# Transformer block with expert routing on one core: new places for the last sequences, a search with both candidates at hand, adds by half

## Chip, cores and metric

The kernel runs on one core of a Trainium2 chip. The metric is the device time of one execution in microseconds; the time before is the median of 3 runs. All 128 partitions are used, all data is float32 unless said otherwise.

## What is computed

```
x: 16 sequences x 256 tokens x 256;   H=16 heads of 64;   E=8 experts, hidden 1024
h     = layernorm(x)*g + b + silu(t) @ W_ada.T + b_ada
q,k,v = h @ Wqkv.T ;  q, k normalised per head
x     = x + softmax(q k' / 8) v @ Wout.T
gate  = softmax(x @ Wgate.T)                   # 4096 tokens x 8 experts
vals, idx = top_k(gate.T, 4096/8)              # every expert takes its 512 best tokens
y     = gelu(layernorm(x[idx]) @ fc1.T + b1) @ fc2.T + b2
out   = x.at[idx].add(y * vals)
```

The choice of the experts needs the gates of all tokens, so it can't begin in full before the last sequence is through the attention.

## The kernel before

**Stages.** The first part works through 16 sequences of 256 tokens (two tiles of 128). For each one `First` normalises and transposes x; `Group` (b, g, t) makes one 512-wide block g of q, k or v for tile t, groups 0 to 3 with square, sum, power (POOL), scaling and transposes, groups 4 and 5 (the values) with a copy alone; `Quad` (b, d) handles four heads in two pairs i of two heads j: scores (TensorE, PE in the profile), maxima (VectorE, DVE), exponentials (ScalarE, ACT), normalising (GpSimd, POOL), transposes, copies and the product with v; `Tail` (b, t) projects, adds x, writes the result to `out` and its normalised form to `xn_dram`, and computes the gates of the tile. In `EARLY` sequences three quarters of the projection are issued ahead of the rest.

**Two routings.** Each expert's 512 tokens are found in two halves of 256. The `first` routing uses the gates of tiles 0 to 29 alone (sequences 0 to 14), so it can run beside the attention of sequence 15; the `second` uses all tiles without those chosen. There are 16 jobs (lines 862 to 985), eight experts for each routing. A job compares places with a row of lane numbers (`onehot`, 30 or 32 tiles), turns that into a list of 256 token numbers with small matmuls (`list_matmul`, `take`), gathers their rows (`gather`, two indirect DMAs issued by POOL), transposes them, runs `up`, `gelu`, `down`, `finish` in two halves i of 128 tokens, and adds each half to `out` (`scatter`, an indirect DMA with addition, issued by POOL).

**The search** (lines 773 to 798) finds for every expert the bits of the value that 256 gates reach, in 30 steps from bit 29 to bit 0. `compare` counts on each partition how many of 256 values reach the candidate, `count` adds up the 16 partitions of an expert with a 128x128 matmul, `drop` turns a count below 255.5 into the bit to take back, and `step` takes it back and sets the next one. All four follow from each other. `masks`, `totals`, `place`, `turn_places` and `split` then give every token its place in the list.

**The order.** Within the first part and up to the first job, the order in which each engine gets its work is written out by hand. Every step has a place, a number; the steps are sorted by it (line 1068) and issued in that order, and each engine takes its own in that order. The numbers give the order alone, they set no times. `STEADY` (line 137) has the places of one sequence, shifted by `PERIOD` for each; `START` and `END` (lines 182 and 252) replace parts of them for the first and last sequences; `GATES`, `TURN`, `SEARCH`, `PLACE`, `LIST`, `UP`, `DOWN` and `SCATTER` (lines 332 to 372) have those of the routing and the first job. The jobs from 1 on run in a loop of 16 slots each (line 1101), with the second routing's steps, the next job's lists and its gather laid into the slots.

**Buffers** are rings: a tile takes the next buffer of its tag and waits until the last readers of it are done. Tags that matter here: `mm` (3 PSUM banks: projections, transposes, counts), `sc` (4: scores and transposed scores), `po` (1), and in SBUF `pr` (6: exponentials), `prT` (5: their transposes), `tok` (2), `xn` (3).

Of the kernel before, what the change touches and what calls it, by code (L numbers as in the profile page):

```python
# [18 lines left out]
P = 128  # L19
# [7 lines left out]
TB = N // P  # L27
# [16 lines left out]
def kernel(  # L44
# [35 lines left out]
    def rsqrt(dst, src):  # L80
# [13 lines left out]
    )  # L94
    below = const.tile([P, P], BF16, name="below")
# [156 lines left out]
    END = {  # L252
        13: dict(
            tail=((785.465, 790.273, 798.692, 815.100, 809.231, 833.838, 858.249, 860.611), (801.111, 811.928, 832.334, 851.976, 852.521, 857.274, 860.648, 863.953)),
        ),
        14: dict(
            quad={
                (0, 0): (778.689, 786.219, 823.152),
                (0, 0, 0): (779.682, 781.429, 786.791, 815.299, 818.486),
                (0, 0, 1): (785.912, 785.925, 792.535, 808.580, 817.952),  # L260
                (0, 1): (780.096, 783.733, 823.483),
                (0, 1, 0): (781.545, 781.892, 784.628, 788.947, 788.970),
                (0, 1, 1): (780.101, 782.800, 786.708, 786.733, 788.171),
                (1, 0): (797.364, 818.438, 836.328),
                (1, 0, 0): (800.501, 805.864, 819.296, 829.860, 830.258),
                (1, 0, 1): (800.411, 814.443, 822.953, 828.276, 828.813),
                (1, 1): (793.490, 829.748, 838.784),
                (1, 1, 0): (796.388, 796.418, 830.890, 834.362, 838.122),
                (1, 1, 1): (808.778, 813.542, 829.820, 831.934, 838.359),
                (2, 0): (820.804, 836.676, 852.048),  # L270
                (2, 0, 0): (828.203, 828.813, 838.415, 843.722, 847.331),
                (2, 0, 1): (827.939, 828.914, 836.722, 843.910, 849.000),
                (2, 1): (836.374, 842.713, 852.072),
                (2, 1, 0): (836.407, 839.805, 842.769, 848.474, 850.007),
                (2, 1, 1): (839.520, 841.416, 848.115, 848.519, 850.465),
                (3, 0): (816.908, 832.905, 857.083),
                (3, 0, 0): (825.275, 825.873, 838.515, 849.510, 853.000),
                (3, 0, 1): (827.433, 827.464, 834.209, 851.571, 852.526),
                (3, 1): (838.557, 848.820, 857.138),
                (3, 1, 0): (842.137, 843.903, 849.558, 853.124, 855.600),  # L280
                (3, 1, 1): (838.661, 846.376, 854.896, 856.165, 856.629),
            },
            out=(833.850, 847.258, 852.123, 857.223),
            tail=((862.946, 865.847, 868.980, 875.067, 865.880, 866.612, 872.508, 873.385), (858.831, 861.745, 877.140, 877.177, 862.888, 865.191, 867.264, 869.065)),
        ),
        15: dict(
            group={
                (0, 0): (783.010, 784.168, 792.362, 806.317, 814.099, 816.308, 819.667, 798.729),
                (0, 1): (830.066, 833.953, 850.378, 857.740, 857.952, 870.574, 874.791, 839.548),
                (1, 0): (879.001, 881.846, 885.813, 890.395, 890.820, 899.277, 903.588, 882.489),  # L290
                (1, 1): (873.858, 878.170, 878.690, 878.937, 883.088, 887.096, 887.770, 879.768),
                (2, 0): (846.402, 853.106, 854.291, 858.091, 859.371, 870.406, 875.263, 852.946),
                (2, 1): (840.588, 856.986, 858.168, 861.123, 862.155, 868.313, 873.733, 844.023),
                (3, 0): (890.733, 891.793, 895.647, 895.684, 895.713, 917.885, 917.990, 894.050),
                (3, 1): (881.675, 882.780, 889.034, 892.080, 894.627, 906.787, 911.766, 884.681),
                (4, 0): (888.740, 890.011),
                (4, 1): (863.214, 868.004),
                (5, 0): (923.865, 925.480),
                (5, 1): (924.711, 926.046),
            },  # L300
            quad={
                (0, 0): (877.464, 881.499, 926.628),
                (0, 0, 0): (879.672, 880.455, 885.321, 920.421, 922.538),
                (0, 0, 1): (879.870, 880.809, 887.655, 912.768, 921.958),
                (0, 1): (877.518, 892.971, 933.343),
                (0, 1, 0): (886.956, 891.463, 894.729, 911.136, 911.826),
                (0, 1, 1): (880.898, 888.187, 894.314, 911.428, 916.354),
                (1, 0): (895.648, 919.627, 937.995),
                (1, 0, 0): (898.733, 909.723, 928.093, 930.689, 932.290),
                (1, 0, 1): (910.215, 915.043, 924.694, 928.544, 932.034),  # L310
                (1, 1): (886.728, 916.952, 939.979),
                (1, 1, 0): (887.974, 905.007, 923.144, 927.338, 929.333),
                (1, 1, 1): (892.287, 897.473, 926.382, 928.417, 929.117),
                (2, 0): (923.105, 929.115, 953.105),
                (2, 0, 0): (923.819, 925.246, 929.628, 941.427, 943.494),
                (2, 0, 1): (926.871, 927.001, 942.982, 945.434, 945.886),
                (2, 1): (921.492, 928.553, 954.846),
                (2, 1, 0): (926.000, 926.034, 939.614, 940.072, 943.252),
                (2, 1, 1): (924.318, 925.786, 942.242, 945.444, 951.283),
                (3, 0): (931.133, 940.346, 955.254),  # L320
                (3, 0, 0): (936.244, 936.261, 940.865, 941.536, 950.189),
                (3, 0, 1): (933.464, 935.504, 943.785, 944.131, 949.789),
                (3, 1): (937.165, 948.250, 957.499),
                (3, 1, 0): (938.436, 940.374, 948.920, 954.409, 955.964),
                (3, 1, 1): (940.955, 942.777, 948.685, 953.607, 955.715),
            },
            out=(934.112, 945.132, 954.889, 957.518),
            tail=((961.580, 961.705, 961.951, 972.971, 962.994, 969.038, 969.773, 970.133), (961.977, 963.425, 970.214, 973.543, 969.153, 973.476, 975.274, 976.692)),
        ),
    }  # L330
    EARLY = {14: (859.048, 858.196,), 15: (957.531, 960.238,)}
    GATES = ((865.946, 872.056, 872.537, 895.813,), (873.513, 875.766, 877.480, 896.008,))
    TURN = (877.896, 880.780,)
    LOAD = (862.948, 961.979)
    SEARCH = (
        (880.819, 881.055, 881.404, 881.710), (882.829, 883.509, 886.236, 886.333),
        (887.758, 887.777, 888.291, 888.656), (888.696, 889.378, 891.481, 891.532),
        (891.823, 892.179, 892.583, 894.026), (895.504, 895.899, 896.433, 897.275),
        (897.999, 902.133, 902.702, 903.674), (910.101, 910.322, 914.650, 914.946),
        (915.318, 915.341, 915.350, 915.983), (916.961, 917.286, 917.306, 918.504),  # L340
        (919.277, 920.204, 920.381, 920.683), (920.702, 920.727, 920.758, 921.907),
        (922.078, 922.144, 922.719, 922.794), (923.075, 923.211, 923.878, 923.905),
        (924.099, 924.525, 925.286, 925.814), (925.990, 926.221, 926.333, 926.641),
        (926.653, 927.067, 927.185, 927.194), (927.246, 928.070, 928.254, 928.471),
        (929.054, 929.057, 929.362, 929.575), (930.411, 931.087, 931.232, 931.596),
        (932.027, 932.536, 932.959, 933.097), (933.383, 933.445, 933.785, 934.727),
        (934.977, 937.418, 937.926, 938.225), (938.272, 939.383, 939.547, 940.683),
        (940.952, 940.980, 941.209, 942.937), (942.957, 942.999, 943.081, 943.091),
        (943.308, 943.939, 944.131, 944.157), (944.158, 944.713, 948.920, 948.933),
        (949.194, 950.535, 950.850, 950.862), (951.462, 952.102, 952.117, 952.284),  # L350
    )
    PLACE = (952.741, 953.958, 955.045, 956.213, 956.540, 970.822,)
    LIST = (
        dict(gives=957.438, onehot=(956.590, 957.558, 956.649, 957.964, 958.690, 958.856,),
             matmul=(957.536, 958.538, 958.607, 958.768, 958.802, 959.218,),
             then=(959.465, 959.489, 962.176, 962.208,)),
        dict(gives=958.877, onehot=(959.876, 961.470, 960.649, 958.698, 962.036, 961.622,),
             matmul=(960.722, 961.809, 961.857, 962.038, 963.442, 963.636,),
             then=(965.066, 965.769, 967.569, 971.532,)),
    )  # L360
    UP = (
# [827 lines left out]
```

## Time and profile before

| | us |
|---|---|
| median of 3 runs | 1214.87 (1214.84 to 1214.93) |
| the profiled execution | 1212.76 |
| its span, first to last instruction | 1210.8 |
| PE busy | 1168.7 (97%) |
| DVE, ACT, POOL busy | 764.4, 618.2, 591.3 |
| first search, first comparison to the masks | 879.68 to 927.14 |
| first `up` matmul of job 0 | 949.43 |

The page divides the span into 40 equal slices of some 30 us. A digit is the busy share of an engine in tenths; `PEclk` is the clock that TensorE was granted. Every row of a timeline has its start in us from the span's start, its length, the engine, the line of the kernel, the operation, and in brackets the idle time ahead of it with what ended that. PEld is the load of a matmul's stationary operand, which may run beside the matmul before.

### The profile page before, as it was taken

The numbers are of one execution on the slowest core, as the hardware profiler recorded it, in microseconds if no ns is written. First come the engines' busy times: TensorE is split into PE (matmuls) and PEld (weight loads), VectorE is DVE, ScalarE is ACT, GpSimd is POOL, SyncE is SP. The second block draws the span as 40 slices with busy tenths as digits, with TensorE's granted clock in tenths as the row PEclk, the third lists the DMA queues.
The fourth block names the chain that finished last, engine by engine and source line by source line (L and its number), as shares of the span: only waits on it lengthen the run. The fifth ranks groups of instructions, "written<-read, shape, count | busy, mean of one in ns | idle before, by whom it ended". The sixth has DMA issues, their size and how long they took to land. (4 is left out here: it accounts for less than half of the span.)

```text
span 1210.8 us, 19463 instructions
## 1 busy us (share of the span) xinstructions
PE 1168.7 (97%) x6784; PEld 813.0 (67%) x6784; DVE 764.4 (63%) x2244; ACT 618.2 (51%) x1701; POOL 591.3 (49%) x818
## 2 busy tenths in 40 slices
PE   6999999999999999999999999999987989999996
PEld 3556666667575666666666657567744778888885
DVE  7656665757665656666575666565578557875541
ACT  2665565555555555556555555556564233333331
POOL 4654555545455555555554545555574233333332
PEclk9999999999999999999999999999989899999999
DMA  5000000000000000000000000000200356666661
GB/s 184 1 1 5 22 6 23 9 18 14 14 14 14 27 1 27 6 22 6 22 10 18 14 14 14 14 19 14 97 0 2 114 178 182 179 182 181 183 184 25
DMA packets 46738, 62.40 MB, mean 52 GB/s; under 512 B 3888, under 2 KB 39984, under 8 KB 46640
## 3 DMA queue, kind: packets, MB, share of 16 engines
q1 hardware_dynamic: 39808, 52.70, 12.8%
q0 software_dynamic: 6144, 8.39, 3.8%
q8 instruction: 54, 0.88, 0.3%
q14 instruction: 44, 0.36, 0.1%
q10 hardware_dynamic: 688, 0.06, 0.0%
HBM read 48.56 MB, written 12.58 MB: 50 GB/s over the span
## 5 line engine op out<-in xcount | busy, mean ns | idle before, releaser
L608 POOL TENSOR_SCALAR pr<-pr,sums 128x256 f32<-128x256 f32 x512 | 238.7, 484 | 277.1 <-DVE sums L604 258.7
L506 PE MATMUL pm<-wq,hT 128*128 128x512 f32 x768 | 355.0, 601 | 5.2 <-DMA wq<-in_wqkvT 3.1
L597 ACT ACTIVATE pr<-sc,nmax 128x256 f32<-128x256 f32 x512 | 236.4, 476 | 162.8 <-DVE nmax L588 148.3
L82 POOL TENSOR_TENSOR ss<-ss,neghalf 128x8 f32<-128x8 f32 x128 | 210.4, 1648 | 96.0 <-DVE ss L527 93.2
L506 PEld LDWEIGHTS pm<-wq,hT 128*128 128x128 f32 x768 | 137.5, 191 | 147.7 <-issue 137.5
L588 DVE TENSOR_REDUCE nmax<-sc 128x2 f32<-128x512 f32 x256 | 164.6, 682 | 45.6 <-PE sc L581 45.5
L523 DVE TENSOR_REDUCE ss<-sq 128x8 f32<-128x512 f32 x128 | 87.4, 683 | 106.0 <-ACT sq L519 105.9
L617 PEld LDWEIGHTS pp<-ident,pr 128*128 128x128 f32 x1024 | 118.3, 143 | 34.9 <-issue 19.6
L617 PE MATMUL pp<-ident,pr 128*128 128x128 f32 x1024 | 137.6, 274 | 3.3 <-ACT pr L597 2.5
L635 PE MATMUL po<-prT,v 128*64 128x256 f32 x1024 | 137.6, 391 | 0.7 <-ACT oT L645 0.7
L581 PE MATMUL sc<-kT,qT 64*128 64x256 f32 x1024 | 131.2, 394 | 0.0
L519 ACT ACTIVATE sq<-pm 128x512 f32<-128x512 f32 x128 | 77.1, 602 | 90.5 <-PE pm L506 89.3
L659 PE MATMUL pw<-wo,oT 128*128 128x256 f32 x512 | 119.4, 386 | 0.0
L971 PE MATMUL py<-w,hid 128*128 128x256 f32 x512 | 118.7, 385 | 0.0
L955 PE MATMUL ph<-xT,w 128*128 128x256 f32 x512 | 118.3, 384 | 0.0
L581 PEld LDWEIGHTS sc<-kT,qT 64*128 64x128 f32 x1024 | 94.7, 188 | 35.0 <-issue 23.7
L981 POOL DMA_INDIRECT out<-y,idx x32 | 51.4, 1606 | 125.2 <-DVE y L978 61.9
L597 ACT ACTIVATION_READ_ACCUMULATOR pr<-sc,nmax 128x1 f32 x512 | 105.8, 207 | 0.0
L971 PEld LDWEIGHTS py<-w,hid 128*128 128x128 f32 x512 | 96.0, 192 | 13.5
L659 PEld LDWEIGHTS pw<-wo,oT 128*128 128x128 f32 x512 | 96.2, 193 | 13.2 <-issue 0.8
L625 DVE COPY prT<-pp 128x512 f32<-128x512 f32 x112 | 76.9, 687 | 43.6 <-PE pp L617 42.7
L955 PEld LDWEIGHTS ph<-xT,w 128*128 128x128 f32 x512 | 94.9, 190 | 13.4 <-ACT xT L943 0.2
(118 smaller groups left out, 1262.7 us busy)
## 6 DMA issues: line engine op xcount, KB each, us to landing
w<-in_fc2T SPq DMA_DIRECT2D x16, 1024.0 KB, 5.5
w<-in_fc1T SPq DMA_DIRECT2D x16, 1024.0 KB, 8.1
xs<-in_x SPq DMA_DIRECT2D x16, 256.0 KB, 2.7
out<-tok SPq DMA_DIRECT2D x32, 128.0 KB, 1.7
xn_dram<-tn SPq DMA_DIRECT2D x32, 128.0 KB, 1.7
wq<-in_wqkvT SPq DMA_DIRECT2D x6, 512.0 KB, 8.4
b<-in_b2s SPq DMA_DIRECT2D x16, 128.0 KB, 8.1
wo<-in_woutT SPq DMA_DIRECT2D x1, 1024.0 KB, 10.4
```

Of the source, the lines that this page charges most:

```text
L82: nc.gpsimd.tensor_tensor(dst, src, neghalf[:, : src.shape[1]], ALU.pow)
L506: nc.tensor.matmul(self.pm, hTs[self.b][:, c, bass.ts(self.t, P)], wq[:, c, bass.ts(self.g, GW)], start=(c == 0), stop=(c == DC - 1),)
L523: nc.vector.tensor_reduce(self.ss[:, 0, :], self.sq.rearrange("p (h d) -> p h d", d=HD), AX.X, ALU.add,)
L581: nc.tensor.matmul(self.sc[i, j][:, t, :], qTs[self.b][rows, hp, bass.ts(t, P)], kTs[self.b][rows, hp, :], start=True, stop=True,)
L588: nc.vector.tensor_reduce(self.nmax[i, j], self.sc[i, j], AX.X, ALU.max, negate=True)
L597: nc.scalar.activation(self.pr[i, j][:, t, :], self.sc[i, j][:, t, :], AF.Exp, bias=self.nmax[i, j][:, t : t + 1], scale=1.0, accum_out=se ...
L608: nc.gpsimd.tensor_scalar(self.pr[i, j][:, t, :], self.pr[i, j][:, t, :], self.sums[i][:, 1, j, t : t + 1], 1.0, ALU.mult, ALU.mult,)
L617: nc.tensor.transpose(self.pp[i, j][:, c, bass.ts(t, P)], self.pr[i, j][:, t, bass.ts(c, P)], ident,)
L635: nc.tensor.matmul(self.po[j * HD : (j + 1) * HD, i, :], vs[self.b][:, c, bass.ts(4 * self.d + 2 * i + j, HD)], self.prT[i, j][:, c, :], s ...
L659: nc.tensor.matmul(self.pw, oTs[self.b][:, hp, bass.ts(self.t, P)], wo[:, hp, :], start=(hp == 0), stop=(hp == HP - 1),)
L955: nc.tensor.matmul(self.ph[f], self.w1[:, c, bass.ts(f, P)], self.xT[:, c, :], start=(c == 0), stop=(c == DC - 1),)
L971: nc.tensor.matmul(self.py[i], self.hid[:, f, bass.ts(i, P)], self.w2[:, f, :], start=(f == 0), stop=(f == FC - 1),)
```

## The change

Five things are changed together.

1. New places for the last four sequences. Sequences 0 to 11 keep theirs. Sequence 12 has a new tail, sequence 13 new quads and a new tail, sequence 14 everything, sequence 15 everything. `GATES`, `TURN`, `SEARCH`, `PLACE`, `LIST`, `UP` and `DOWN` have new places throughout.
2. The search of the first routing: `count`, `drop` and `step` become `count_over`, `either` and `decide`. The count is doubled and has 510 taken off, so that it is at least 2 where 256 values reach the candidate and at most 0 where they don't; `either` makes both next candidates from the present one; `decide` picks one of them with a maximum and a minimum. The second routing keeps the old steps.
3. The lists: the list matmuls of job 1 are issued in one block of 30, and job 2's comparisons in three blocks of 11 tiles instead of one of 30.
4. Each half of job 0 is added to `out` at the place at which it is finished, half 1 ahead of half 0; before, both adds were placed after everything else, half 0 first.
5. More buffers: `xn` 4, `pr` 8, `prT` 8, `tok` 3.

```diff
+    twice = const.tile([P, P], BF16, name="twice")
+    nc.gpsimd.tensor_scalar(twice, block, 2.0, None, ALU.mult)
+    less = const.tile([1, 1], BF16, name="less")
+    nc.gpsimd.memset(less, -2.0 * (CAP // 2 - 1))
...
     SEARCH = (
-        (880.819, 881.055, 881.404, 881.710), (882.829, 883.509, 886.236, 886.333),
...
+        (915.830, 916.092, 916.183, 917.655), (919.245, 919.328, 919.498, 920.432),
...
+        (937.975, 939.958, 937.941, 940.394), (940.424, 940.468, 941.936, 941.964),
...
+        (951.225, 951.311, 951.757, 953.021), (953.529, 954.238, 953.182, 955.515),
...
+        (972.936, 973.254, 972.067, 974.926), (974.965, 975.145, 975.081, 975.172),
...
-    DOWN = ((977.710, 981.210), (974.250, 978.517))
-    SCATTER = 987.575
+    DOWN = ((1020.447, 1020.575), (1014.649, 1019.361))
...
+            def count_over(self, n):
+                self.pc = ps.tile([P, 1], F32, tag="mm", bufs=3, name="pc")
+                nc.tensor.matmul(self.pc, ones[:1, :P], less, start=True, stop=False)
+                nc.tensor.matmul(self.pc, twice, self.cnt, start=False, stop=True)
+
+            def either(self, n):
+                self.next = []
+                for name, op in (("keep", ALU.bitwise_or), ("drop", ALU.bitwise_xor)):
+                    new = bit.tile([P, 1], I32, tag=name, name=name)
+                    nc.vector.tensor_scalar(
+                        new, self.cand, 0 if name == "keep" else 1 << n, (1 << n) >> 1,
+                        op, ALU.bitwise_or,
+                    )
+                    self.next.append(new)
+
+            def decide(self, n):
+                keep, drop = self.next
+                self.cand = bit.tile([P, 1], I32, tag="cand", name="cand")
+                nc.vector.tensor_scalar(
+                    self.cand.bitcast(F32), self.pc, drop.bitcast(F32), keep.bitcast(F32),
+                    ALU.max, ALU.min,
+                )
...
-            at(p, *(partial(f, n) for f in (first.compare, first.count, first.drop, first.step)))
+            at(p, *(partial(f, n) for f in (first.compare, first.count_over, first.either, first.decide)))
...
+        for k, place in enumerate(LIST[2]["onehot"]):
+            if k == 0:
+                at([place], jobs[2].gives)
+            at([place], partial(jobs[2].onehot, 11 * k, 11 * k + 11))
...
+            w = NT if len(p["matmul"]) == 1 else 5
...
+            for k, place in enumerate(p["matmul"]):
+                at([place], partial(a.list_matmul, w * k, w * k + w))
...
-            at([SCATTER + i * 0.1], partial(jobs[0].scatter, i))
-        at([min(t[5] for t in END[B - 1]["tail"])] * 2, jobs[2].gives,
-           partial(jobs[2].onehot, 0, NT))
+            at(DOWN[i][1:], partial(jobs[0].scatter, i))
```

The four entries shown of the new `SEARCH` come in pairs of steps, from bit 29 down: the rows shown hold steps 29 and 28, 23 and 22, 17 and 16, 9 and 8. The places of sequences 12 to 15 are too many to show; from them come, on PE in order, between the last scores of sequence 14 (d 3, i 1) and its last transposes: before, a product, group 2 t 1, two transposes, group 2 t 0, four transposes, two products; after, two products, group 2 t 0, five transposes, two products.

## The prediction

> **What bounds the kernel now.** I read the page first, its slices before its groups.
>
> ```profile
> PE   6999999999999999999999999999987989999996
> PEclk9999999999999999999999999999989899999999
> ```
>
> TensorE (PE) is busy in nine tenths or more of nearly every slice, at full clock. So the stages before about 870 us and after 1000 us can only be shortened by less PE work, and no PE work is taken away here. What can be won lies in slices 30 to 33. The answer by stretches gives them (PE, weight load, DVE, ACT, POOL, then the clock):
>
> ```profile
> 878.40:897.00 18.60, 14.17 (x74) 7.99 (x73) 16.44 (x59) 14.57 (x45) 17.15 (x20) 1.00 0.00 0
> 897.00:905.00 8.00, 7.35 (x27) 4.21 (x27) 4.97 (x21) 2.63 (x7) 5.46 (x14) 0.57 0.00 0
> 905.00:927.10 22.10, 16.97 (x114) 10.12 (x114) 16.51 (x73) 13.33 (x41) 7.35 (x16) 1.00 0.01 1
> 934.20:949.40 15.20, 12.77 (x94) 9.95 (x92) 11.16 (x62) 0.59 (x2) 9.08 (x13) 0.78 0.09 26
> 970.00:990.00 20.00, 16.89 (x101) 14.28 (x100) 10.04 (x52) 5.79 (x13) 8.07 (x10) 0.91 0.50 133
> ```
>
> From 878.4 to 927.1 us the first search runs beside the attention of sequence 15. PE idles there for 10.2 us of 48.7, and does 8 us at about half clock. The waits of that stretch name the search:
>
> ```profile
> DVE drop L788 <- PE pc L783: 6.8, 16, 1.3
> PE pc L783 <- DVE reach L776: 7.8, 9, 1.7
> ```
>
> The two engines wait for each other, in a chain of 30 steps (47.5 us from the first comparison, 879.68, to the masks, 927.14). One step with nothing else in it is, on DVE:
>
> ```profile
> 898.12 0.48 DVE L776 TENSOR_SCALAR_CACHE_REDUCE reach<-gT,cand 128x256 bf16<-128x256 f32 x1
> 898.53 0.09 DVE L776 DVE_READ_ACCUMULATOR reach<-gT,cand 128x1 bf16 x1
> 898.87 0.16 DVE L788 TENSOR_SCALAR drop<-pc 128x1 int32<-128x1 f32 x1 [0.26 <-PE pc L783]
> 899.06 0.16 DVE L795 SCALAR_TENSOR_TENSOR cand<-drop,cand 128x1 int32<-128x1 int32 x1
> 899.25 0.48 DVE L776 TENSOR_SCALAR_CACHE_REDUCE reach<-gT,cand 128x256 bf16<-128x256 f32 x1
> ```
>
> That is 1.13 us: 0.49 compare and read, 0.26 until the count is there, 0.19 to the next start for L788, 0.19 for L795. Later PE waits once more, behind POOL (timeline, first column the start):
>
> ```profile
> 967.61 1.67 POOL L981 DMA_INDIRECT out<-y,idx  x1 [13.80 <-DVE gates L719]
> 975.68 1.57 POOL L981 DMA_INDIRECT out<-y,idx  x1 [6.41 <-DMA out<-y,idx]
> 978.83 1.15 POOL L927 DMA_INDIRECT xg<-xn_dram,idx  x1
> 981.91 0.30 PE L936 MATMUL px<-ident,xg 128*128 128x128 f32 x1 [2.17 <-DMA xg<-xn_dram,idx]
> 983.14 0.90 PE L936 MATMUL px<-ident,xg 128*128 128x128 f32 x3 [0.93 <-DMA xg<-xn_dram,idx]
> ```
>
> The second add of job 0 stands on POOL until the first has landed, and the gather of job 2, whose list was ready at 972.0, stands behind it.
>
> [...] eight score matmuls took 2.08 us at 898.76 and 1.13 at 882.35; twelve projection matmuls took 5.33 at 940.57. But no single PE gap there was over 1.72 us[...]. [...] the first add, with job 2's weights issued at 966.49, needed 8.07 us against a median of 3.9. [...]
>
> **The change, part by part** (span of the profiled execution).
>
> *Set-up.* One 128x128 POOL operation (row nearest: 0.35, L87) and one memset (0.10, L78). POOL ends its set-up at 4.60 and waits until 5.14 for DVE, so 0.45 is covered: 0, at most 0.5 where it isn't. Loads of x for 14 and 15 move earlier on an SP queue that mostly waits: 0.
>
> *Places before the search.* Counted by steps, PE has the same 220 us between the first scores of sequence 11 and the turn, in both orders; tails 12 and 13 move later, quads and projections of 13 and 14 move between them. PE was at 79.67 of 80 from 780 to 860, so nothing is to be won but the 0.34 in 840 to 860. Risk: of the stage from the first scores of 14 to the turn, PE's share rises from 55 to 64 us and ACT's from 41 to 46, so the ratio falls, and after the last scores of sequence 14 PE has 7.8 us before it needs their last transposes (9.2 before). The chain there is 0.7 maxima, about 3.6 for four pairs of exponentials, 1.9 on POOL, and a few 0.58 copies: 7 to 8. The larger buffer counts (pr 8, prT 8, tok 3, xn 4) allow for that. I take 0, between -0.5 and +2.5.
>
> *The search.* L795 goes: 30 times 0.19. Two operations come, which need only the old candidate and follow each other at 0.08 (an independent pair does so: 887.80 and 887.88 in DVE's timeline). That is 0.16 where both are independent, up to 0.38 where they are not. In a bare step they fill the 0.26 that DVE waits anyway: 0.49 + 0.26 + 0.19 = 0.95, or 1.07 at the dear end. By the new places 15 steps are bare (22 to 18, 15, 12 to 10, 5 to 0): 15 times -0.18 = -2.7. In the other 15 a maximum or a statistic already fills the wait: -0.03 each, -0.5. In steps 23, 16 and 9 the pair stands ahead of the comparison, in the chain: +0.5. The count is now two matmuls; no row shows a second one, but one with its weight load costs PE 0.1 (97 ns load, partly hidden), and it only counts where PE is late, after scores, products or groups: 9 steps, +0.9 (0 to 3). Together -1.8. The order of PE's work is nearly the old one, with one difference: two scores and two value projections stood in four steps running (17 to 14 in the old numbering), which at half clock took 2.2 to 2.6 us each where 1.4 to 1.9 would do; now they alternate with lighter pieces. The old excess is 1.8; I count half, -0.9. Three waits of PE's transposes for ACT (2.2 in this stretch) may shorten with more buffers: -0.3. Search: **-3.0**, between -6.5 and +0.5.
>
> *Lists and first gather.* Masks to split are unchanged (6.5 us). Job 0's list still waits for POOL's ten comparisons with 0.62 apiece (6.24, until 940.46); that cover is not touched. Job 1's lists are now one block behind job 0's transposes, so PE reaches those about 0.7 earlier: **-0.7**. If job 1's list is later, its gather is too (PE waited 0.57 and 0.40 for it): -2 to +1. Job 2's lists move from one piece of 5.05 to three of 1.9 among the last tail's steps on DVE; PE's gate of tile 31 waits for one of these, behind 3.7 us of the down projection: 0.
>
> *The adds.* The first half is finished at 963.83 (DVE), the second at 967.31. The first add is now queued then: at 963.9 in place of 967.6, ahead of the weights issued at 966.49, so it should land after about the median 3.9, near 968. The second add starts at 968 to 969 and lands behind the weights, but only job 1's adds at 981.6 wait for it. Queued behind it on POOL are the last gate parts (2 us) and the gather of job 2, so 972.0 to 974.5 in place of 978.83 to 981.3. With the 6.2 us that a gather took under a weight load, the rows are there at 978.5 to 980.5; PE wants them at 979.74. PE's 2.17 + 0.93 = 3.1 go, and with them the drop of the clock from 983.17 to 986.58 (3.41 at half: 1.7): 4.8. I leave 0.3: **-4.5**, between -5 and -1.5. What is late next: nothing, PE is full from 990 on.
>
> *Sum.* 0 + 0 - 3.0 - 0.7 - 4.5 = -8.2. The span is 1210.8 and the profiled execution's own time 1212.76, so 1204.6 for that execution. The median of the runs is 1214.87, 2.1 more; carried over: 1206.7, said as **1207**.
>
> **The rivals.**
> - *The search stays.* DVE is the bound there: 37.9 busy of 48.7, and it loses only 0.9 in all; what PE gets done per step is set by DVE's maxima. For: 16 steps were filled before and 15 are now. Against: 6.8 us of DVE's waits are for the count. Then only adds and lists remain: -5, 1210 (1210 to 1212.5).
> - *More comes free.* PE keeps its clock through the search and the lists (half clock at 897.8 to 904.7 and 938.8 to 945.6, 3.4 each), and the search nears the sum of its floors, 41 us: -6.5 - 3 - 4.5 = -14, 1201 (1199 to 1203.5). Against: the lists' wait for POOL is the same[...].
> - *Slower: PSUM held before the search.* The projection results of sequence 15, g0 t1 and g2 t1, now wait long for their squares on ACT, whose queue has seven copies and four exponentials ahead. They hold up to two of the three buffers, and PE stands behind in its queue, with sequence 14's output projection. Each us that ACT lags is a us of PE[...]. ACT is busy 15.3 of 20 at 840 to 860. It decides from about 10.5 us of new PE idle there: -8.2 + 10.5 + 1.7 for the clock is +4, 1219. Against: by the places, 3.9 us of PE work stand between the two partial projections, against 1.0 of ACT.
> - *No difference.* Some of that idling and a longer search eat the gain: 1212.5 to 1217.3.
>
> **How the numbers follow.** My forecast (1203.5 to 1210) has 0.58, the search that stays 0.14, more 0.09, no difference 0.06, slower 0.13. Within 0.2% is 2.4 us, about what a measurement of this kernel can tell from no change. Faster 0.81, same 0.06, slower 0.13. The range 1200.5 to 1213.5 takes in the forecast, the search that stays, most of the larger gain and a little of no difference; slower is left out.
>
> **What would show it.** In the trace after: bare steps at 0.95 (the pair inside the wait), not 1.13; the search at about 44.5; two adds some 4.5 apart, the first at once after the first half; no PE wait for xg of job 2 and clock 1.00 in that stretch; before the turn no PE wait of a microsecond. The prediction is wrong if the pair costs more than 0.3, if PE idles before the search, or if job 2's gather still comes late behind the second add.

## The result and the profile after

The changed kernel takes **1201.62 us** (median of 4 runs, 1200.95 to 1202.32) against 1214.86 us (4 runs beside them, 1213.28 to 1214.93): a ratio of 0.9894, 95% interval 0.9877 to 0.9911, so 1.1% faster. Forecast was 1207, with 1200.5 to 1213.5 as the range. The profiled execution after took 1200.95 us with a span of 1199.23 (before: 1212.76 and 1210.84), so its span is 11.6 us shorter.

Five points in both traces cut that difference: the first comparison of the search (L776, now L826), the masks, the first up product of job 0, that of job 1, and the end. "Rest" is from job 1's first up product to the end. The row "forecast" has the terms of the prediction's sum.

| | to the first comparison | search | lists (masks to job 0's up) | job 0 (its up to job 1's up) | rest |
|---|---|---|---|---|---|
| before | 879.7 | 47.5 | 22.3 | 16.9 | 244.5 |
| after | 878.0 | 41.6 | 21.1 | 19.2 | 239.4 |
| difference | -1.7 | -5.8 | -1.2 | +2.3 | -5.2 |
| forecast | 0 | -3.0 | -0.7 | 0 | -4.5 |

The page's slices of after, PE's busy share and the clock that it was granted, show the two gaps of before closed but for one slice:

```profile
PE   6999999999999999999999999999999899999996
PEclk9999999999999999999999999999999899999999
```

The answer by stretches (sum and share per engine in the order PE, weight load, DVE, ACT, POOL, then clock, DMA share and GB/s) tells what lies in that slice (929.4 to 959.4 us):

```profile
878.00:919.60 41.60, 37.48 (x243) 22.73 (x243) 37.21 (x178) 30.51 (x91) 28.72 (x50) 1.00 0.00 1
927.00:940.70 13.70, 11.73 (x91) 9.30 (x90) 10.12 (x59) 0.79 (x2) 7.42 (x10) 0.75 0.08 21
940.70:951.00 10.30, 8.57 (x45) 7.21 (x44) 6.83 (x37) 5.79 (x12) 3.34 (x4) 1.00 0.80 280
951.00:959.90 8.90, 8.90 (x37) 7.57 (x37) 3.22 (x16) 0.43 (x1) 1.66 (x1) 0.81 0.09 18
959.90:980.00 20.10, 20.10 (x129) 17.38 (x128) 12.97 (x66) 9.17 (x17) 8.08 (x10) 1.00 0.66 191
```

The search (first line) runs at full clock now, with 4.1 us of PE idle where there were 10.2. The lists (second line) still hold 6.8 us of half clock, and a new piece stands at job 0's down product (fourth line). The last line is the place where PE stood for job 2's rows: no idle, clock 1.00.

In the search the two engines wait less for each other. PE's and DVE's waits between 878.0 and 919.6 us, with sum, times and longest:

```profile
PE pc L857 <- DVE reach L826: 3.7, 12, 0.8
DVE cand L872 <- PE pc L857: 1.4, 6, 0.3
```

Before these were 7.8 and 6.8. One bare step of the new search on DVE (start, duration):

```profile
893.78 0.48 DVE L826 TENSOR_SCALAR_CACHE_REDUCE reach<-gT,cand 128x256 bf16<-128x256 f32 x1
894.18 0.08 DVE L826 DVE_READ_ACCUMULATOR reach<-gT,cand 128x1 bf16 x1
894.18 0.15 DVE L863 TENSOR_SCALAR keep<-cand 128x1 int32<-128x1 int32 x1
894.25 0.14 DVE L863 TENSOR_SCALAR drop<-cand 128x1 int32<-128x1 int32 x1
894.52 0.28 DVE L872 TENSOR_SCALAR cand<-pc,drop,keep 128x1 f32<-128x1 f32 x1
894.84 0.48 DVE L826 TENSOR_SCALAR_CACHE_REDUCE reach<-gT,cand 128x256 bf16<-128x256 f32 x1
```

From comparison to comparison it is 1.06 us, not the 0.95 of the forecast. The pair lies wholly in the wait for the count, as expected. The decision takes 0.28, and the next comparison starts 0.31 or 0.32 after it, where 0.19 was taken from L788.

The adds came out nearly as described. POOL in the trace after:

```profile
957.28 1.66 POOL L1058 DMA_INDIRECT out<-y,idx  x1 [11.34 <-DVE gates L748]
962.24 1.57 POOL L1058 DMA_INDIRECT out<-y,idx  x1 [3.30 <-issue]
965.77 1.19 POOL L1004 DMA_INDIRECT xg<-xn_dram,idx  x1 [0.53 <-DVE chunk L958]
```

The first add is issued 0.3 after its half is finished (956.98), the second 4.96 later, and the gather of job 2 follows 8.5 us after the first add (before: 11.2). PE takes up its rows at 973.17 without a wait.

What the sum of the forecast leaves at nothing is the wait of PE for job 1's rows, which it named as a risk (before, then after):

```profile
957.20 0.30 PE L936 MATMUL px<-ident,xg 128*128 128x128 f32 x1 [0.57 <-DMA xg<-xn_dram,idx]
957.89 0.55 PE L936 MATMUL px<-ident,xg 128*128 128x128 f32 x3 [0.40 <-DMA xg<-xn_dram,idx]
949.35 0.30 PE L1013 MATMUL px<-ident,xg 128*128 128x128 f32 x1 [1.56 <-DMA xg<-xn_dram,idx]
949.83 0.55 PE L1013 MATMUL px<-ident,xg 128*128 128x128 f32 x3 [0.17 <-DMA xg<-xn_dram,idx]
```

PE waits 1.73 in place of 0.97, and from 951.17 to 954.58 its clock is at half, so that the first half of the down product takes 5.31 us where the second takes 3.70.

### The profile page after: what moved, and what is told of

It is laid out like the page before. It is cut to its first block, busy times and chain, and to the rows that moved or that the text cites. A ratio compares the mean times of both kernels' runs of the same rounds, so it can differ in the third digit from the quotient of the medians.

```text
span 1199.2 us, 19564 instructions
## 1 busy us (share of the span) xinstructions
PE 1169.5 (98%) x6814; PEld 814.2 (68%) x6814; DVE 765.0 (64%) x2274; ACT 618.8 (52%) x1701; POOL 593.5 (49%) x820
## 5 line engine op out<-in xcount | busy, mean ns | idle before, releaser
L631 PE MATMUL sc<-kT,qT 64*128 64x256 f32 x1024 | 128.7, 390 | 0.0
L1039 ACT ACTIVATE hid<-ph,vec 128x256 f32<-128x256 f32 x128 | 60.3, 474 | 85.8 <-PE ph L1032 74.4
```

The lines of the kernel that those rows point to most:

```text
L631: nc.tensor.matmul(self.sc[i, j][:, t, :], qTs[self.b][rows, hp, bass.ts(t, P)], kTs[self.b][rows, hp, :], start=True, stop=True,)
```

## The experiments

Two theories stood against each other after the traces were compared. **Order:** the search gained by the order of the work around it and by the buffers, and the exchange of its operations does little. **Operations:** the shorter chain made the gain. Beside these, the adds and the buffer counts were tried alone; part 3 of the change, the lists in blocks, was only ever moved together with the places. The stages of all kernels (us, of the profiled execution), with the median of all runs of each:

| kernel | median | first comparison at | search | lists | job 0 | rest |
|---|---|---|---|---|---|---|
| before | 1214.86 | 879.7 | 47.5 | 22.3 | 16.9 | 244.5 |
| after | 1201.62 | 878.0 | 41.6 | 21.1 | 19.2 | 239.4 |
| before, new operations of the search | 1219.90 | 880.3 | 46.7 | 22.8 | 19.3 | 245.4 |
| before, adds by half | 1208.42 | 879.9 | 47.5 | 22.3 | 16.9 | 239.4 |
| before, new buffer counts | 1208.74 | 878.3 | 45.1 | 24.9 | 17.0 | 244.5 |
| before, new places and buffer counts | 1208.08 | 878.1 | 44.5 | 21.4 | 19.6 | 242.5 |
| after, old operations of the search | 1202.34 | 875.2 | 44.8 | 20.0 | 21.0 | 239.4 |
| after, old buffer counts | 1217.03 | 885.0 | 53.0 | 21.6 | 19.1 | 239.3 |
| after, old places | 1205.04 | 877.6 | 46.2 | 21.3 | 17.6 | 239.5 |
| after, new count for pr alone | 1202.75 | 878.0 | 43.8 | 21.5 | 17.5 | 239.4 |
| after, other decision | 1198.68 | 876.7 | 40.7 | 21.4 | 17.4 | 239.4 |
| after, job 1 early | 1198.86 | 875.4 | 41.6 | 22.2 | 15.5 | 239.3 |
| both, and one-hots moved | 1195.01 | 877.3 | 40.7 | 20.0 | 15.4 | 239.5 |
| the same, pairs behind | 1194.66 | 877.4 | 40.7 | 20.0 | 15.4 | 239.3 |

The time of one kernel varies by some us (after itself by 1.4, the kernel with the new operations alone by 6.5), so the times are compared by their ratios, each against the kernel before on the same chip. The stages of a row are those of one execution, and they hold whatever half clock that execution met: the runs of the new operations alone took a mean clock from 0.991 (1215.1 and 1216.3 us) down to 0.984 (1221.6).

**The search's operations alone**, on the kernel before, with both candidates made right behind the comparison (cut to the arguments that differ):

```
-at(p, ... (first.compare, first.count, first.drop, first.step))
+at((p[0], p[1], p[0], p[2]), ... (first.compare, first.count_over, first.either, first.decide))
```

> Only the search's operations are exchanged (counts over the ones matrix, both next candidates, one decision); places, buffers and adds are the old ones. Theory 'order': the operations alone shorten a bare step from 1.13 us only to the 1.06 that the trace after shows, and leave the filled steps as they are, so 15 to 20 steps by 0.07 to 0.1: 1 to 2.5 us, 1212.4 to 1213.9; the half clock near 898 to 905 us stays. Theory 'operations': the search is a chain on DVE and PE and most of its 5.8 us come with the shorter chain: 1209 to 1210.5, and the half clock goes.

Measured: ratio 1.0048 [1.0030, 1.0066], **slower**; neither theory had that. The search itself is 0.7 shorter, as "order" said, with bare steps of 1.06, but it doesn't carry over: the first comparison comes 0.6 later, the lists and the rest take 0.6 and 0.9 more, and the wait for job 1's rows grew:

```profile
958.22 0.30 PE L967 MATMUL px<-ident,xg 128*128 128x128 f32 x1 [1.18 <-DMA xg<-xn_dram,idx]
959.06 0.55 PE L967 MATMUL px<-ident,xg 128*128 128x128 f32 x3 [0.54 <-DMA xg<-xn_dram,idx]
```

That is 1.72 in place of 0.97; 3.4 us of half clock follow at 960.3, as they do after the 1.73 of the changed kernel, and not after the 0.97 of before. The profiled execution was among the shorter ones (1216.27 at a mean clock of 0.991; others up to 1221.68 at 0.984). By these clocks the longest runs had about 17 us more at half clock (an estimate: 0.007 of 1218 us, twice); where it lay is in no trace.

**The adds alone**, on the kernel before:

```
-at([SCATTER + i * 0.1], partial(jobs[0].scatter, i))
+at(DOWN[i][1:], partial(jobs[0].scatter, i))
```

> Only the adds are queued by half, everything else is as before. Theory 'adds by themselves': the gather of job 2 is no longer behind the first add's landing, the wait of PE for its rows (3.1 us) and the half clock after it (1.7 us) go: 1209.5 to 1211. Rival 'the adds gain only because job 0 ends earlier or job 2's list is laid in three pieces': the gather of job 2 then waits for its list or for the second add, and the time is 1212.5 to 1214.9.

Measured: 1208.42, ratio 0.9965 [0.9952, 0.9977], a little more in the median than expected. In the trace the stages up to job 1 agree within 0.3 and the rest falls from 244.5 to 239.4, and so it does in every kernel with adds by half. The adds need nothing of the other parts, and the rival falls.

**The buffer counts alone**, on the kernel before (the counts, not the lines of the code):

```
-xn 3, pr 6, prT 5, tok 2
+xn 4, pr 8, prT 8, tok 3
```

> Only the buffer counts are the new ones (xn 4, pr 8, prT 8, tok 3). Theory 'buffers': the three waits of PE at 66 and 80 us (2.7 us) go, and with the half clock near 26 to 30 us that came with them the steady part begins 1.2 us earlier: 1213.5 to 1213.9; rival 'the start moved for another reason, the two new operations of the set-up': 1214.9, and PE still waits at 66 and 80 us.

Measured: 1208.74 (1205.19 to 1211.50), ratio 0.9948 [0.9934, 0.9962]: **far more than either said**. The waits of PE between 40 and 100 us of the kernel before, and its wait for the exponentials in the search, were

```profile
PE pq L548 <- ACT v L515: 1.5, 2, 1.2
PE pp L617 <- issue: 0.8, 1, 0.8
PE pm L506 <- ACT qT L560: 0.5, 1, 0.5
PE pp L617 <- ACT pr L597: 2.2, 3, 0.8
```

and with the new counts PE has none of these; the first comparison comes 1.4 earlier, although this trace has 3.4 us of half clock at 26.8 us where before has none. The search takes 45.1 in place of 47.5, with 12.5 us of it at half clock. The profiled execution is the longest of its six (1211.50, mean clock 0.985), with 6.8 us of half clock from 921.1, at the end of the search and in the lists; the two shortest, 1205.2 and 1205.3, had 0.991. So much of the gain in the median lies in executions that were not traced.

**The new places with these buffers**, old operations, both adds at the end:

> The new places and buffer counts with the old operations of the search and the adds at the end. Theory 'order': the places bring most of the search's 5.8 us, 1.7 us before it and 1 us in the lists, and lose 2 us where job 1's rows are late: 1207.5 to 1210. Theory 'operations': the search stays at 46 to 47 us, and the time is 1211.5 to 1214.

Measured: 1208.08, ratio 0.9956 [0.9943, 0.9969], in the range of "order". But it is not better than the buffers alone. Search 44.5, and already the job 0 of 19.6. PE's and DVE's waits in its search up to 919.6 us (it ends at 922.6) are

```profile
PE pc L833 <- DVE reach L826: 6.3, 13, 0.9
DVE drop L838 <- PE pc L833: 3.6, 13, 0.9
```

and 6.8 us at half clock stand at 893.4. Steps 17 and 16 in it, at half clock, took 2.60 and 2.33 where the same two take 1.78 and 1.53 in after.

**The changed kernel with the old operations** (drop and step at the place of the decision):

> The changed kernel with the old operations of the search (drop and step at the place of the decision). Theory 'operations need the places': at the new places the new operations are worth what lies between 44.45 us (new places, old operations) and 41.62 us, so the search takes about 44.5 us and the time is 2.8 us up, 1203.5 to 1205. Theory 'operations are worth what they bring at the old places': 0.7 us, 1202 to 1203. The difference to the kernel with the places alone (1208.1) is then that of the adds at the new places, 3 to 5 us.

Measured: the search 44.8, so 3.2 more, the size that "operations need the places" said, but 10.2 us at half clock are back in it, and what of the 3.2 is theirs can't be told apart in this trace. The time is 1202.34, ratio 0.9901 [0.9886, 0.9917], which the changed kernel's interval overlaps: in the whole time the gain of the operations isn't separable. In this trace the first comparison came 2.8 us earlier for a reason that has nothing to do with the edit (see the end), and job 0 is 1.9 longer, with 6.8 us at half clock. Against the places alone the rest is 242.5 to 239.4: the adds are worth 3.1 there.

**The changed kernel with the old places**, that is, the new operations, adds and buffers on the kernel before (the lists are its old ones):

> The old places with everything else of the change: the new buffer counts, the new operations of the search and the adds by half. Theory 'buffers and operations make the search': 41.5 to 43 us for the search, and the time 1202 to 1205. Theory 'the places make it': the search takes 44 to 46.5 us as with the old places and new buffers (45.07) or with the old places and new operations (46.73), and the time is 1205.5 to 1210.

Measured: 1205.04 (1203.55 to 1208.91), ratio 0.9929 [0.9910, 0.9948]. The search is 46.2, so "the places make it" for the search; the time falls between the two ranges, because job 0 is 17.6 here and not 19. Half clock stands in the search (895.8, 6.8 us).

**The changed kernel with the old buffer counts:**

> The changed kernel with the old buffer counts (xn 3, pr 6, prT 5, tok 2). Theory 'buffers': the start loses its 1.4 us again (PE waits at 66 and 80 us), and in the search PE waits for ACT's exponentials or copies again: 1204 to 1208, the search 43 to 45 us. Rival 'the new places need no more buffers, only the start does': 1202.8 to 1203.5, the search below 42.

Measured: **1217.03**, ratio 1.0019 [1.0009, 1.0029]: slower than before, and beyond what "buffers" had said. ACT in its search:

```profile
ACT pr L647 <- PE pp L667: 8.6, 2, 4.5
```

An exponential waits for a transpose that is late, since the transposes free the buffers of pr; in after this group is not among ACT's waits of the search. The search takes 53.0, and the first comparison comes 7.0 later: 1.3 of that are there before the 20th tail's gate product (648.9 against 647.6), and PE idles 3.5 between 750 and 885 us where it has no idle from 750 to 878 in after. Of the search, 22.5 us are at half clock in this trace, but all sixteen runs are slow against after: the shortest took 1213.1 at a mean clock of 0.992, that of after's profiled run.

**Only pr with its new count:**

```
-xn 4, prT 8, tok 3
+xn 3, prT 5, tok 2
```

> The changed kernel with the new count for pr alone (8) and the old ones for xn, prT and tok. With all old counts ACT waited 9.1 us between 780 and 885 us, and 8.6 us in the search, for PE's transposes ahead of an exponential, that is, for a buffer of pr to come free. Theory 'pr': the waits are gone with pr alone, the search is 41.5 to 42.5 us and the time 1200.5 to 1203.5. Rival 'prT (or tok, xn) too': part of the loss stays, the search at 43 to 53 us, 1205 to 1216.

Measured: 1202.75, ratio 0.9910 [0.9894, 0.9927], inside the range for pr and overlapping the changed kernel's. The start is that of after and PE has no wait between 40 and 100 us. The search is 43.8, more than expected of pr alone, with 6.8 us at half clock again at 892.7. So pr is the count that decides in the time. Whether the other three give the clock in the search or chance does stays open.

**The decision in another form:**

```
-nc.vector.tensor_scalar(cand, pc, drop, keep, ALU.max, ALU.min)
+nc.vector.scalar_tensor_tensor(cand, pc, drop, keep, ALU.max, ALU.min)
```

> The changed kernel; the decision is one scalar_tensor_tensor (one per-lane scalar and one tensor of one element) in place of a tensor_scalar with two per-lane scalars. Theory 'the second per-lane scalar costs': the decision takes 0.16 in place of 0.28, a bare step 0.95 in place of 1.06, and the search loses 1 to 3 us: 1198.6 to 1200.6. Rival 'reading PSUM or the float form costs': still 0.28, 1201.6.

Measured: 1198.68, ratio 0.9871 [0.9855, 0.9888], search 40.7. The step on DVE:

```profile
889.15 0.48 DVE L826 TENSOR_SCALAR_CACHE_REDUCE reach<-gT,cand 128x256 bf16<-128x256 f32 x1
...
889.89 0.22 DVE L872 SCALAR_TENSOR_TENSOR cand<-pc,drop,keep 128x1 f32<-128x1 f32 x1
890.14 0.48 DVE L826 TENSOR_SCALAR_CACHE_REDUCE reach<-gT,cand 128x256 bf16<-128x256 f32 x1
```

The decision takes 0.22 and the bare step 1.00. The second per-lane scalar is half of the surplus: of 0.12 over the old drop, 0.06 go. The other half stays with the form that has one; the old drop, with constants, reads PSUM too and takes 0.16, and the old step, a scalar_tensor_tensor with a constant on SBUF, takes 0.16 as well (L788 and L795 of before). So neither PSUM nor the instruction itself explains it; the type, float here and integer there, was not varied. The search is 0.9 shorter; the other 2 us of the median are not the decision's. This trace has no half clock in job 0, which takes 17.4 in place of 19.2, although PE waits for job 1's rows as long as in after:

```profile
947.55 0.79 PE L1013 MATMUL px<-ident,xg 128*128 128x128 f32 x4 [1.71 <-DMA xg<-xn_dram,idx]
```

So do the kernels with pr alone and with the old places: waits of 1.79 and 1.68, no half clock, 17.5 and 17.6.

**Job 1 early:** its list is counted ahead of the last quarter of a projection, and taken and gathered ahead of the last tails' statistics; the two tails exchange places.

```
-onehot=(1004.079, 999.874, 1002.078, 1001.570, 1004.476, 1002.735,),
-matmul=(1005.317,), then=(1009.609, 1009.667, 1010.783, 1015.258,)
+onehot=(1002.800, 999.874, 1002.078, 1001.570, 1002.850, 1002.735,),
+matmul=(1003.000,), then=(1004.900, 1004.910, 1010.783, 1015.258,)
```

> The changed kernel with job 1's list counted ahead of the last quarter of a projection, its numbers taken and its rows fetched ahead of the tails' statistics; the two last tails exchange their places. Theory 'job 1 is late by its place on DVE and PE': its rows are there 3 us sooner, the waits of 1.73 us ahead of its transposes and the half clock after them (1.6 us) go: 1198.3 to 1199.8, and from job 0's first up to job 1's 16.0 to 17.0 us in place of 19.15. Rival 'the gather is slow because of job 1's weights on the DMA engines, wherever it is queued' or 'PE idles after job 0's transposes instead': 1200.8 to 1202.5.

Measured: 1198.86, ratio 0.9873 [0.9859, 0.9887]. POOL's gather and PE's transposes of job 1:

```profile
937.79 0.95 POOL L1004 DMA_INDIRECT xg<-xn_dram,idx  x1 [4.74 <-DVE w L999]
...
946.21 0.60 PE L1013 MATMUL px<-ident,xg 128*128 128x128 f32 x4
```

No wait, no half clock after it; job 0 falls from 19.15 to 15.45, even less than expected, while the lists, which now hold job 1's count, take 1.1 more. Against the three traces that have the wait but no half clock (17.4 to 17.6), some 2 of these 3.7 us are the wait's, and about 1 remains after the lists. Job 1's lateness was its place in the queues of PE and DVE, not the transfer.

**All of it:** both edits, and five of POOL's ten comparisons for job 0's list given to DVE, which also makes one of job 1's blocks later. In after PE waited for POOL with

```profile
PE pls L985 <- POOL oh L976: 1.8, 5, 0.5
```

> The changed kernel with three things: the decision as scalar_tensor_tensor, job 1's list and rows early, and five of the ten comparisons that POOL makes for job 0's list given to DVE. If they add: search 0.9 less (40.7 us), job 1 2.6 less, and the wait of PE for POOL's comparisons (1.8 us) goes because POOL then ends near 929 and DVE near 930.7 us: 1.6 less; 1194.5 to 1197.5. Rival 'the list is then late for another reason (the rows still need 6 us after it, and PE has only 7 us of projections to lay over it)': the lists stay at 21 to 22 us and the time is 1196.5 to 1199.

Measured: **1195.01**, ratio 0.9839 [0.9823, 0.9856]. They add: PE no longer has this wait, and the lists take 20.0 with 3.4 in place of 6.8 us at half clock.

**The same with the pair behind the comparison in steps 23, 16 and 9:**

> The kernel with the three things, and in steps 23, 16 and 9 the pair of candidates behind the comparison in place of ahead of it. The prediction's term: three times 0.16 us less in the chain, the search 0.5 us shorter than in the same kernel without this, the time 0.5 us less. Rival: in these steps DVE's other work or PE's waits anyway, and search and time stay within 0.2 us.

Measured: 1194.66, ratio 0.9827 [0.9808, 0.9845], the search 40.7 as without it. From comparison 24 to comparison 23 it takes 1.67 in place of 1.80, and from there to the next 1.37 in place of 1.24: the 0.13 come back at once. The rival holds.

## Why the prediction was right, and where it was not

The sign, the range and the places of the gain were right. But 1201.6 lies below what the prediction called its own forecast, 1203.5 to 1210; it lies in the band of a rival to which it gave 0.09, "more comes free". The sum (-8.2 against -11.6 in the span) hides errors that partly cancel, and how much of the surplus is chance was not shown. By its own steps:

- **Set-up 0:** right for PE, though not on the ground given. POOL's new multiplication takes 0.56 where a row of 0.35 was taken, and POOL's set-up ends 0.6 later; the cover of 0.45 didn't hold. But PE's first projections wait for their weights anyway (with the operations alone they start at 11.13, before at 10.98). That this kernel is 0.6 late from there on is mostly their length, 8.93 in place of 8.49, as full clock came at 14.8 us and not at 13.8.
- **"The stages before about 870 us can only be shortened by less PE work":** wrong, and the error is in how the slices were read. A 9 means 90% or more; PE waited 2.8 us between 60 and 90 us under a row of nines. The larger counts took these waits away (-1.4 at the first comparison, shown by the buffers alone). Ahead of the search the forecast counted the larger buffers as permission for the new places only, and gave them no term.
- **Places before the search 0, with a risk of up to 2.5:** right for the kernel as changed. The first comparison comes as early with the buffers alone (878.3) as with places and buffers (878.1). The slower rival, PSUM buffers held ahead of the turn, didn't come: no PE wait before it. But a slower end did exist at this place, in other buffers: with the old counts the same places give 1217, and with that of pr alone made new 1202.75.
- **The search -3.0:** mis-sized, -5.8, and for another reason than the sum gives. The term for the bare steps (0.95) failed at the decision, which was priced with the row of L788, 0.19 to the next start; it takes 0.31. The sum's dear end, 1.07, comes near the measured 1.06 by luck: it stood for a pair of operations that lag, and the pair does not. So the operations alone give 0.7 at the old places and, with the new buffers, nothing there (45.1 to 46.2). The term "two matmuls, +0.9" wasn't seen by itself. "The pair ahead of the comparison, +0.5" is 0. The two small terms are where the gain was: "three waits of PE's transposes for ACT, -0.3" stands for the buffers, of which the search shows 2.4 in one trace; "half of the old excess at half clock, -0.9" stands for a clock that is now whole. At the new places the search is 2.8 to 3.2 shorter with the new operations; two steps at half clock hold 1.6 of that. In these traces no part makes it alone: the five that have the places, the four counts and the new operations together run the search at full clock, and the nine others, before included, have half clock in it. But each is one execution. The sum of PE's idle time in the search doesn't sort them: the kernel with pr alone has 3.4 us of it and half clock, after has 4.1 and none. What does was not shown, and chance may have a part in the full clock of this execution.
- **Lists and first gather -0.7, "if job 1's list is later, its gather is too":** the lists gained 1.2 (with the same 6.8 us of half clock, three other traces with the new places have 21.4 or 21.5, so 0.8 to 1.2). The named risk came, at +2.3 in job 0: the wait grew by 0.8, and half clock followed, which the forecast priced nowhere. In three traces with the same wait it did not follow, and job 0 rose by 0.5 to 0.7 only. That the wait comes from job 1's place in the order, moving it showed.
- **The adds -4.5:** right in mechanism, -5.2 (3.1 at the new places alone). The 0.3 left over for a remainder was not needed.

Of the rivals, "more comes free" (1201) came nearest, at 0.09 of chance: PE keeps its clock through the search, though not through the lists, whose wait for POOL was read correctly as untouched. That wait went only when comparisons were moved to DVE.

## What to carry to other kernels

A digit of nine in the slices can hide idle time (here 2.8 us between 60 and 90): ask for the waits of each stage before saying that only less work can help, and price a larger buffer count as an edit of its own. Price a new instruction by a row with the same kinds of operands, and count a wait together with what PE's clock may do after it: here, of eight traces with a wait of 1.7 to 2.2 us for job 1's rows, half clock followed in five, and in after it cost another 1.6. When an order is changed, look at once at what the moved step was queued ahead of; job 1's list cost up to 2.3 us, and a few places in a table gave it back.

## What the runs showed that was not expected

- A tensor_scalar with two per-lane scalars on one element per lane took 0.28 us, a scalar_tensor_tensor with one of them 0.22, either form with constants in their place 0.16 (L788 and L795 of before).
- The clock differs between kernels whose instructions there are the same. In after, 3.4 us at half clock begin at 26.2 us and a projection of four products takes 3.57; in the kernel with job 1 early the same projection takes 1.98, and all that follows is 2.6 us earlier (first comparison 875.4 against 878.0). Of that, 0.9 is there already at the projection before it, since full clock was first granted at 14.2 in place of 15.9. That alone is more than most terms of the sum, so stages were compared, not spans. Half clock has pieces of 3.4 us (in after from 26.16 and from 951.17) and of 6.8 (in after from 930.69, in before from 897.83). Two stretches of after, then two of the kernel with job 1 early (PE's busy time first; the clock is the third number from the end):

```profile
22.74:26.16 3.42, 1.37 (x7) 0.68 (x6) 3.33 (x7) 1.38 (x2) 2.17 (x2) 1.00 0.00 0
26.16:29.57 3.41, 3.41 (x6) 1.23 (x6) 3.27 (x9) 0.06 (x1) 1.96 (x3) 0.50 0.00 0
21.00:24.42 3.42, 1.92 (x8) 0.64 (x6) 3.28 (x9) 0.86 (x2) 2.11 (x3) 1.00 0.00 0
24.42:27.83 3.41, 2.84 (x14) 1.80 (x15) 3.27 (x8) 1.34 (x3) 2.78 (x3) 1.00 0.00 0
```

  PE was busy for 1.37 of 3.42 us ahead of the half clock of after, and for 1.92 of 3.42 in the kernel that kept full clock; no run varied this by itself.
- Half clock came after many small waits as well: in the lists of after no wait of PE exceeds 0.5 us and yet 6.8 us at half follow, with ten comparisons on POOL; with five it is 3.4. PE was busy for 2.6 of the 3.4 us before.
